# A two-layer adaLN kernel on one core: the hand-over from attention to the experts, and the normalisation in front of it

## The chip, the cores and the metric

The kernel runs on one core of one Trainium2 chip. The metric is the time of one execution in microseconds on the device; less is better. All data are float32, apart from small float16 tables of zeros, ones and counts that the routing uses. The engines named below are PE (TensorE, matrix products), DVE (VectorE), ACT (ScalarE), POOL (GpSimd) and SP (SyncE, which here only issues DMAs). PE needs two records in the trace for one float32 product, so the counts of float32 products in the profile are twice those in the code.

## The reference, cut to what matters

`x` has 4 batches of 1024 tokens of 256 features. Every layer has an attention part and a feed-forward part, each behind a layer norm that is modulated by rows computed from a condition `c`:

```python
mod = (silu(c) @ wmod).reshape(4, 6, 1, 256)   # shift, scale, gate, for both parts
h = layernorm(x) * (1 + ca) + sa
x = x + ga * L0_attn(h, queries, combiners)     # linear attention, 4 heads of 64
h = layernorm(x) * (1 + cb) + sb
x = x + gb * L0_ffn(h, W1, b1, W2, b2, Wr, br)  # 8 experts, the best 2 of each token
mod = (silu(c1) @ wmod1).reshape(4, 6, 1, 256)  # "layer 1's modulation rows"
x = x + ga1 * L1_attn(...)                      # a gated MLP over chunks of 128 tokens, in sequence
x = x + gb1 * L1_ffn(...)                       # 8 single matrices, the best 2 of each token
```

The attention has no softmax, so for each batch it comes down to a Gram matrix of `h` per head, a product with the combiners and one with the queries, and then one 128x128 product per 128 tokens. In `L0_ffn` an expert is a 256x1024 matrix with a ReLU and a 1024x256 matrix. Which two experts a token gets depends on the data.

## The kernel before, in words

**Tiles.** The 4096 tokens are 32 tiles of 128: 8 chunks `c` for each of 4 batches `b`, in the order `c * 4 + b`. Chunks 0 to 3 (`g = 0`, "half 0") are tiles 0 to 15, chunks 4 to 7 (`g = 1`, "half 1") are tiles 16 to 31.

**The prologue.** It ends at about 104 us. It is a list of pieces, each with an engine, an estimated duration, what it comes after, the buffer slots that it holds, and a rank. The class `Plan` simulates the engines with these estimates, always taking the ready piece of lowest rank, and writes the pieces out in the order in which the simulation began them; the engines then run exactly that order (`manual_schedule`). `FIRSTS[b]` and `SECONDS[b]` are the ranks of a batch's two halves of work:

- `first_half(b)`: `normalised` (below), `to_features` (transposes on PE, shift and scale on ACT), `to_tokens` (transposed back), the Gram matrix, `head_t1` (two products of a 128x128 block-diagonal matrix `gd` with the combiners, line 1289) and `head_m`.
- `second_half(b)`: the products with `md`, the sums into `x_sb` (DVE), `normalised` again, `to_features`, the router's product (line 194, in four column tiles of 32), and `route` on DVE, which picks two experts per token. Batch 3 (`SPLIT`) routes its two halves apart, four tiles each; the others route eight tiles at once. The tokens are stored to `h_rows` in DRAM, one DMA for each `g` of a batch, and `mark` stores their routing data.

`normalised` does for each group of four tiles: `bn_stats` and `bn_aggr` for each tile (lines 1097 and 1098, DVE), then the variance plus epsilon into `ln_v` (line 1101, DVE), the square root (line 1105, ACT), a reciprocal and one Newton step (lines 1109 to 1116, DVE), and last the scaling of the tiles, two on POOL (line 1126) and two on ACT (line 1128). There are 16 such groups: four batches, two halves of chunks, two norms.

**The hand-over.** Each half's routing table is turned round by `turn` (PE), copied by `turned` (ACT, `pairs`) and `counted` (DVE, `more`). When both are there, `bases` (PE) and `begin` (ACT) give blocks 0 and 1 their limits; both belong to expert 7. `sought(j)` finds the 128 tokens of block `j`: `reach` (DVE, line 817, one instruction for each half), `look` (PE, line 847), `find` (DVE, lines 860 and 869). `first_block` then fetches the rows of block 0 with an indirect DMA on POOL, which waits for `find` and for all entries of the list `stores`, turns them (PE, line 1562), copies them (ACT, line 1674), and starts the products `hidden` (line 1610) and `values` (line 1634). Meanwhile DVE works out which expert each later block has: `whole_blocks`, `with_halves`, `close_staged`, then `across` on PE (line 749), `limits`, and `sought(2)`. Two kinds of PE work fill holes: 12 pieces of one product and 12 of two products of a tile of ones at low rank (`kept_busy`, line 1033), some of them with an earliest planned time (`at`), and layer 1's modulation rows (`modulation_rows`, line 1523): 12 products, each 4 rows wide, of 256 columns.

**The experts of layer 0.** A program-order loop runs blocks 0 to `turning - 1`, with `turning = J - LATE`, and a second plan those up to `passed = J - SPARE`. A block is 16 products for `hidden` and 8 for `values`. The weights come by indirect DMA on POOL (line 353) into two buffers each for W1 and W2; both pairs are filled with expert 7's before the loop. In the loop, POOL issues the rows of block 2 first and then block 2's W1. `once(j)` does single things at given blocks; at block 5 it stores the modulation rows to DRAM.

Layer 1 follows from about 590 us, from a plan of its own.

## Time and profile before

| what | value |
|---|---|
| median of 8 runs | 1077.8 us (1075.57 to 1080.38) |
| the profiled execution | 1075.64 us, its span 1073.9 us |
| PE busy over the span | 1038.1 us (97%) |
| DVE, ACT, POOL busy over the span | 602.0, 396.8, 426.7 us |
| granted TensorE clock | 0.995 of full speed |
| the chain that ended last | 33% of the span on PE, 8% on DVE |
| 1408 records of `p_h` (line 1610) and 1008 of `p_y` (line 1634) | 275 and 382 ns each |

Busy times are unions of intervals. The ends of matmuls are modelled, so a full PE column means that PE was not left waiting, not that the array worked at its peak. Idle time before an instruction is shown in square brackets with what ended it. Times within the span count from its start.

### The profile page before, as it was taken

To read this page: it belongs to the slowest core of one execution; us is meant where nothing else is said; L and a number is where in the kernel's file an instruction comes from. 1 tells how busy PE (TensorE), PEld (TensorE's weight loads), DVE (VectorE), ACT (ScalarE), POOL (GpSimd) and SP (SyncE) were. 2 spreads that over 40 slices of the span, in tenths; PEclk is the share of its full clock that TensorE was granted. 3 is DMA by queue.
4 is the path that set the end of the run, shared out by engine and by line. 5 is a ranking of instruction groups with operands and counts; after the bars stand their busy time and mean duration, and the time that the engine had idled before them with its cause. 6 is when DMAs were issued, how large, how long until landed. Compare 5 with 4: busy or idle time off the path is not lost. (4 is left out here: it accounts for less than half of the span.)

```text
span 1073.9 us, 18875 instructions
## 1 busy us (share of the span) xinstructions
PE 1038.1 (97%) x6193; PEld 802.0 (75%) x6193; DVE 602.0 (56%) x2323; ACT 396.8 (37%) x1077; POOL 426.7 (40%) x509
## 2 busy tenths in 40 slices
PE   8999999999999999999999999999999999998993
PEld 5885899989989989989999465564656566646751
DVE  7997343232222222221165588878778726698767
ACT  5766332323332332322253433432224325342521
POOL 3211466546555555544453010110106321574644
PEclk9999999999999999999999999999999999999998
DMA  8604626576543726464171222221014322352534
GB/s 284 239 21 110 216 67 212 203 275 198 178 160 119 237 66 201 120 215 153 31 260 40 72 60 64 62 81 48 18 34 140 111 66 77 106 169 76 161 111 147
DMA packets 94255, 139.81 MB, mean 130 GB/s; under 512 B 31009, under 2 KB 69933, under 8 KB 89542
## 3 DMA queue, kind: packets, MB, share of 16 engines
q0 software_dynamic: 30080, 68.89, 20.3%
q1 hardware_dynamic: 62966, 68.04, 19.9%
q10 hardware_dynamic: 1104, 1.58, 0.4%
q8 instruction: 53, 0.87, 0.3%
q14 instruction: 52, 0.43, 0.1%
HBM read 202.22 MB, written 29.17 MB: 215 GB/s over the span
## 5 line engine op out<-in xcount | busy, mean ns | idle before, releaser
L1622 ACT ACTIVATE hid<-p_h,w 128x128 f32<-128x128 f32 x504 | 144.0, 369 | 300.7 <-issue 194.5
L1634 PE MATMUL p_y<-w,hid 128*128 128x256 f32 x1008 | 230.5, 382 | 0.7 <-DMA w<-in_W,g_wrow 0.7
L2430 PE MATMUL p_u<-hT,a 128*128 128x512 f32 x512 | 229.3, 595 | 0.9 <-ACTq L2395 0.9
L1634 PEld LDWEIGHTS p_y<-w,hid 128*128 128x128 f32 x1008 | 186.9, 190 | 24.6 <-issue 1.0
L2430 PEld LDWEIGHTS p_u<-hT,a 128*128 128x128 f32 x512 | 94.9, 190 | 102.6 <-issue 92.8
L1610 PEld LDWEIGHTS p_h<-xTq,w 128*128 128x128 f32 x1408 | 163.3, 192 | 1.7
L1610 PE MATMUL p_h<-xTq,w 128*128 128x128 f32 x1408 | 164.5, 275 | 0.0
L353 POOL DMA_INDIRECT w<-in_W,g_wrow x124 | 125.7, 1013 | 68.6 <-ACT hid L1622 43.8
L1645 DVE TENSOR_TENSOR y<-p_y,w 128x256 f32<-128x256 f32 x64 | 27.2, 424 | 193.3 <-PE p_y L1634 193.2
L914 POOL DMA_INDIRECT y<-y,g_dest x64 | 66.3, 1036 | 131.4 <-DVE y L1645 72.4
L2478 PE MATMUL p_f<-a,hf 128*128 128x256 f32 x512 | 116.9, 380 | 0.0
L2478 PEld LDWEIGHTS p_f<-a,hf 128*128 128x128 f32 x512 | 95.9, 190 | 18.7 <-issue 6.4
L2526 POOL TENSOR_TENSOR x_sb<-x_sb,step 128x256 f32<-128x256 f32 x32 | 24.8, 775 | 207.4 <-DVE step L2519 164.5
L860 DVE TENSOR_SCALAR_CACHE_REDUCE g_hits<-pm_counts,g_nth 128x128 f16<-128x128 f32 x68 | 23.6, 347 | 89.5 <-PE pm_counts L847 86.3
L1610 PE MATMUL p_h<-xT,w 128*128 128x128 f32 x608 | 71.3, 276 | 0.4 <-DVE xT L1567 0.4
L1610 PEld LDWEIGHTS p_h<-xT,w 128*128 128x128 f32 x608 | 70.3, 192 | 1.2 <-DVE xT L1567 0.6
L2442 ACT ACTIVATE hf<-p_u,decay 128x512 f32<-128x512 f32 x56 | 38.3, 685 | 76.9 <-PE p_u L2430 73.4
L2738 PE MATMUL p_e<-ew,xT 128*128 x256 | 65.0, 385 | 0.3 <-ACT y L2748 0.3
L2446 DVE SCALAR_TENSOR_TENSOR hf<-p_u,decay,hf 128x512 f32<-128x512 f32 x56 | 41.8, 746 | 21.6 <-PE p_u L2430 8.3
L2089 DVE TENSOR_TENSOR h<-h,mod 128x256 f32<-128x256 f32 x128 | 51.4, 423 | 4.1 <-ACT h L2079 2.1
L353 POOL DMA_INDIRECT xg<-ga_rows,ga_row x36 | 34.3, 952 | 45.9 <-DVE ga_row L869 16.4
L2738 PEld LDWEIGHTS p_e<-ew,xT 128*128 128x128 f32 x256 | 44.8, 190 | 8.7 <-issue 2.9
(420 smaller groups left out, 1340.3 us busy)
## 6 DMA issues: line engine op xcount, KB each, us to landing
yg<-y SPq DMA_DIRECT2D x32, 256.0 KB
xTq<-square SPq DMA_DIRECT2D x176, 32.0 KB
ew<-in_W SPq DMA_DIRECT2D x16, 288.0 KB
ga_y<-y SPq DMA_DIRECT2D x36, 128.0 KB
half<-in_W SPq DMA_DIRECT2D x16, 257.0 KB
x_sb<-in_x SPq DMA_DIRECT2D x8, 512.0 KB
h_rows<-xn SPq DMA_DIRECT2D x8, 512.0 KB
hT<-square SPq DMA_DIRECT2D x128, 32.0 KB
```

Of the source, the lines that this page charges most:

```text
L353: return nc.gpsimd.indirect_dma_start(out=dst, out_offset=None, in_=table, in_offset=bass.IndirectOffsetOnAxis(ap=index, axis=0), bounds_c ...
L914: nc.gpsimd.indirect_dma_start(out=table if parts == 1 else table.rearrange("r (i d) -> (r i) d", i=parts), out_offset=bass.IndirectOffset ...
L1610: nc.tensor.matmul(p1[:, i, :], lhsT=w1[:, k * H + m * P : k * H + (m + 1) * P], rhs=xT[k], start=(k == 0), stop=(k == KD - 1),)
L1622: nc.scalar.activation(hid[:, m, :], p1[:, i, :], AF.Relu, bias=w1buf[j % 2][:, KD * H + m : KD * H + m + 1],)
L1634: nc.tensor.matmul(p2, lhsT=hid[:, m, :], rhs=w2[:, m * D : (m + 1) * D], start=(m == 0), stop=(m == KH - 1),)
L1645: nc.vector.tensor_tensor(y, p2, w2buf[j % 2][:, KH * D :], ALU.add)
L2089: nc.vector.tensor_tensor(h, h, mods1[(sc, sh)[i]][:, b, :], (ALU.mult, ALU.add)[i])
L2430: nc.tensor.matmul(pu, lhsT=a[:, k, m * P : (m + 1) * P], rhs=made["n1", c, "hT"][:, k, :, :], start=(k == 0), stop=(k == KD - 1),)
L2442: nc.scalar.activation(made[key, m], made[key, m, 0], AF.Silu, scale=decays[c])
L2446: nc.vector.scalar_tensor_tensor(h, made[key, m, 1], decays[c], h, ALU.mult, ALU.mult)
L2478: nc.tensor.matmul(made[key, "p2", b], lhsT=made[key, m][:, b * P : (b + 1) * P], rhs=a1[:, m, :], start=(m == 0), stop=(m == KH - 1),)
L2738: nc.tensor.matmul(made[key, "p2"], lhsT=made[key, "xT"][:, k, :], rhs=ew_flat[:, bass.ds(made[key, "at"] + k * D, D)], start=(k == 0), st ...
```

## The change

In `normalised`, epsilon is added by the square root itself (as its bias) and inside the Newton step, so the separate `ln_v` instruction is gone, and POOL scales three of the four tiles of each group. The ranks `FIRSTS` and `SECONDS` and several estimated durations are new, so the whole order of the prologue is worked out anew. `head_t1` multiplies only the two diagonal 64x64 quadrants. Blocks 0 and 1 are sought among half 0's pairs alone: `first_bases` and `begin` follow half 0's `turn`, a table `absent` stands in for half 1 in `look`, and the first two fetches wait for half 0's stores only. As expert 7 may have fewer than 256 pairs in half 0, `short` corrects the later blocks for it, and `J` grows by one, as do `LATE` and `SPARE`. The six modulation rows are computed in three column tiles at partitions 0, 32 and 64, in four rounds of three products, and stored by six DMAs.

```diff
-LATE = 16
-SPARE = 8
+LATE = 17
+SPARE = 9
...
-    rows1 = half1[:B, : 6 * D].rearrange("p (i d) -> p i d", d=D)
+    rows1 = {}
+    for i, (t, q) in {2: (0, 0), 0: (1, 0), 1: (2, 0), 5: (0, 1), 3: (1, 1), 4: (2, 1)}.items():
+        rows1[i] = (32 * t, q, half1[32 * t : 32 * t + B, q * D : (q + 1) * D])
...
-            self.n, self.J, self.name = n, blocks_of(n) + (name == "g0"), name
+            self.n, self.J, self.name = n, blocks_of(n) + 2 * (name == "g0"), name
...
+        def first_bases(self, pool):
+
+            K = self.K
+            pt = psum(pool, [K, self.halves], "pm_bases")
+            for h, of in enumerate((below16, same16)):
+                nc.tensor.matmul(
+                    pt[:, h : h + 1],
+                    lhsT=of[:K, :K],
+                    rhs=self.pairs[:K, 0, :1],
+                    start=True,
+                    stop=True,
+                )
+            return pt
...
+            nc.vector.tensor_scalar(
+                self.short,
+                self.pt[:, 2, E - 1 :],
+                float(2 * P),
+                float(2 * P),
+                ALU.min,
+                ALU.subtract,
+            )
+            nc.vector.tensor_tensor(
+                whole[:, :, E - 1 :],
+                whole[:, :, E - 1 :],
+                self.short.unsqueeze(1).to_broadcast([P, 3, 1]),
+                ALU.subtract,
             )
...
+            nc.vector.tensor_scalar(
+                origin[:, 0:1], self.short, -1.0 / P, None, ALU.mult
+            )
+            own7 = origin[:, 2 * E - 1 :: E]
+            nc.vector.tensor_scalar(own7, own7, origin[:, 0:1], None, ALU.add)
...
-        def look(self, pool, reached):
+        def look(self, pool, reached, first=False):
...
-                    rhs=self.more[: self.K, h, :],
+                    rhs=(self.absent if first and h else self.more[:, h, :])[: self.K],
...
     def by_gpsimd(k, b, g, i):
-        return i < 2
+        return i < 3
...
-            if c == cs[-1]:
-                v = tiles["v", key] = pa.tile([P, n], F32, tag="ln_v", name="ln_v", bufs=6)
-                nc.vector.tensor_scalar(v, tiles["mv", key][:, :, 1], EPS, None, ALU.add)
...
-            nc.scalar.activation(y, tiles["v", key], AF.Sqrt)
+            nc.scalar.activation(y, tiles["mv", key][:, :, 1], AF.Sqrt, bias=eps)
...
-            nc.vector.tensor_tensor(t, t, v, ALU.mult)
+            nc.vector.scalar_tensor_tensor(t, mv[:, :, 1], EPS, t, ALU.add, ALU.mult)
...
-    FIRSTS, SECONDS, SPLIT = [0, 1.3, 2.42, 2.65], [1.28, 4.7, 2.66, 4.55], 3
+    FIRSTS, SECONDS, SPLIT = [0, 1.48, 1.79, 1.8], [1.64, 5.29, 3.2, 4.59], 3
...
-                nc.tensor.matmul(
-                    p1[:, j, :],
-                    lhsT=gd[:, j, :],
-                    rhs=comb[:, j, :, :].rearrange("p a g -> p (a g)"),
+                for r in (slice(0, 64), slice(64, P)):
+                    nc.tensor.matmul(
+                        p1[r, j, :],
+                        lhsT=gd[r, j, r],
+                        rhs=comb[r, j, :, :].rearrange("p a g -> p (a g)"),
...
+        if half == 0:
+            ps2 = plan.slot("p1")
...
+            m2 = plan(PE, 0.15, first_bases, after=[of_batch["turned"]], holds=[ps2], rank=-1.6)
+            begun = plan(
+                ACT,
+                0.35,
+                lambda: g0.begin(tiles["first bases"]),
+                after=[m2],
...
+        for col in range(2):
+            for k in range(KD):
+                def mm(col=col, k=k):
+                    for i, (at, q, _) in rows1.items():
+                        if q == col:
+                            nc.tensor.matmul(
+                                tiles["rows1"][at : at + B, q * D : (q + 1) * D],
+                                lhsT=sT1[:, k, :B],
+                                rhs=tiles["wm1"][:, k, i * D : (i + 1) * D],
...
-            POOL, 1.0, lambda: g0.fetch(xgbuf[0], h_rows, 0), after=[found, *stores], rank=-1.6, lag=2.9
+            POOL, 1.0, lambda: g0.fetch(xgbuf[0], h_rows, 0), after=[found, *stores[0]], rank=-1.6, lag=2.9
...
-    d = plan(DVE, 1.6, lambda: g0.limits(pa), after=[m, bs], holds=[ps], rank=-1.0)
+    d = plan(DVE, 1.6, lambda: g0.limits(pa), after=[m, bs, found[0], found[1]], holds=[ps], rank=-1.0)
...
-            nc.sync.dma_start(mod_rows1, rows1)
+            for i in range(6):
+                nc.sync.dma_start(mod_rows1[:, i, :], rows1[i][2])
```

## The prediction

> **What bounds the kernel now.** I read the page first. PE has work almost throughout:
>
> ```profile
> PE 1038.1 (97%) x6193; PEld 802.0 (75%) x6193; DVE 602.0 (56%) x2323; ACT 396.8 (37%) x1077; POOL 426.7 (40%) x509
> ```
>
> PE's idle gaps, added up from its timeline, come to under 3 us between 104 and 594 us. So the experts of layer 0 start when the prologue lets them, and run at PE's pace: whatever moves their start moves the end by as much. The change is all ahead of that start (after it stand six small stores for one). What matters is what bounds the prologue. The busy time by stretches says:
>
> ```profile
> 8.00:20.00 12.00, 10.73 (x75) 7.79 (x74) 10.90 (x51) 6.56 (x12) 4.73 (x41) 1.00 1.09 360
> 20.00:40.00 20.00, 18.76 (x247) 15.83 (x245) 18.36 (x75) 14.03 (x29) 4.39 (x8) 1.00 0.88 331
> 40.00:60.00 20.00, 18.86 (x232) 16.05 (x233) 18.15 (x79) 16.41 (x35) 5.62 (x10) 1.00 0.20 58
> 60.00:80.00 20.00, 19.77 (x250) 17.62 (x247) 17.88 (x67) 14.05 (x29) 3.29 (x6) 1.00 0.08 28
> 80.00:95.00 15.00, 13.45 (x140) 8.79 (x139) 12.75 (x61) 12.39 (x26) 2.20 (x4) 1.00 0.66 156
> ```
>
> The third pair is DVE: 90% in each stretch. The rest is not waiting: in its timeline from 8.0 to 94.9 us all gaps over 0.1 us add up to 0.8 us, and the others are the 0.03 to 0.04 us between dependent instructions. PE looks as full, but 16.8 us of it before 110 us are products of ones (line 1033) and its ends are modelled. DVE bounds the prologue. Its relevant groups between 8 and 95 us:
>
> ```profile
> L1097 DVE BATCH_NORM_STATS2 ln_st<-x_sb 128x6 f32<-128x256 f32 x60 | 24.6, 410 | 0.7 <-DMA x_sb<-in_x 0.4
> ...
> L1113 DVE TENSOR_TENSOR ln_t<-ln_t,ln_v 128x4 f32<-128x4 f32 x16 | 2.8, 173 | 0.5
> ...
> L1101 DVE TENSOR_SCALAR ln_v<-ln_mv 128x4 f32<-128x4 f32 x15 | 2.5, 170 | 0.5
> ```
>
> Then the hand-over, from the timelines of DVE, PE and POOL:
>
> ```profile
> 86.62 0.46 DVE L426 TENSOR_TENSOR r_hit<-r_hit,rank 128x64 f32<-128x64 f32 x1
> ...
> 88.43 0.23 DVE L426 TENSOR_TENSOR r_hit<-r_hit,rank 128x64 f32<-128x64 f32 x1
> ...
> 94.54 0.17 DVE L446 TENSOR_TENSOR g_both<-g_one 128x32 f16<-128x32 f16 x1
> ...
> 96.17 0.74 DVE L817 TENSOR_SCALAR g_reached<-count,g_limit 128x128 f16<-128x128 f16 x4 [0.43 <-ACT g_limit L603]
> ...
> 102.85 0.32 DVE L700 TENSOR_TENSOR g_diagonal<-ident,g_of_p 128x152 f32<-128x152 f32 x1
> ```
>
> ```profile
> 97.46 4.91 PE L1523 MATMUL pm_mod<-wmod,sT 128*4 128x256 f32 x22
> 102.30 0.51 PE L1562 MATMUL pm_x<-ident,xg 128*128 128x128 f32 x2
> ...
> 103.71 1.05 PE L1610 MATMUL p_h<-xg,w 128*128 128x128 f32 x8
> 104.60 0.42 PE L749 MATMUL pm_blocks<-g_diagonal,ones 128*128 128x152 f32 x2
> ...
> 116.90 3.84 PE L1610 MATMUL p_h<-xT,w 128*128 128x128 f32 x32 [0.40 <-DVE xT L1567]
> ```
>
> ```profile
> 98.80 1.15 POOL L353 DMA_INDIRECT xg<-h_rows,g_row  x1 [11.25 <-DVE g_blocks_i L625]
> ...
> 109.54 0.95 POOL L353 DMA_INDIRECT xg<-h_rows,g_row  x1 [8.34 <-DVE g_row L869]
> 110.80 1.03 POOL L353 DMA_INDIRECT w<-in_W,g_wrow  x1 [0.30 <-issue]
> ```
>
> The last route ends at 94.71 us, blocks are sought from 96.17, block 0's rows are asked for at 98.80 and land at 101.8 (DMA completions), PE turns them at 102.30, right behind the modulation rows, and block 0 starts at 103.71. Block 2 (116.90) is the first with new weights: asked for at 110.80, landed at 116.6.
>
> **The prologue, by parts.** *Line 1101 goes.* Where it stands, the next independent DVE instruction starts 295 ns after `bn_aggr`; elsewhere 99 ns after. So it takes 196 ns, 16 times: **-3.1 us**, in an engine that does not wait. The Newton step swaps a TENSOR_TENSOR (173 ns) for the form of its neighbours (163 to 176 ns): 0. The memset of epsilon falls into DVE's idle 3.25 us at 2 us: 0.
>
> *POOL scales 16 more tiles.* They take 563 ns each on POOL, idle for 65 of these 87 us, and leave ACT, where they take 598. Price on DVE: a two-input instruction that meets a scaling lasts longer (the 0.46 above against 0.23; in Newton steps 0.26 to 0.35 against 0.16). I add up some 1.2 us over today's 32 tiles, so 16 more cost **+0.6 us** (0 if they meet none, 1.2 if twice as often). `bn_stats`, the largest row, takes 409 ns under a scaling and 409 without. The Trainium skill (SBUF — State Buffer, "Who interferes with whom") speaks against the move more strongly: of a two-input DVE instruction and a GpSimd one that reads SBUF, the second fully blocks. Taken as a stop of half a scaling, 0.28 us, for each of the 16, that would be 4.5 us, an estimate; the trace shows far less, as most of DVE's time has one SBUF input. A group's scaling now ends after three POOL tiles (1.8 us). In the last group it ended 2.2 us after Newton, as ACT had other work (POOL 86.46 to 87.56, ACT until 88.37): -0.4 to +0.6, I take 0, hidden by routes that DVE does meanwhile; uncovered it would be 0.6.
>
> *`head_t1`.* Four records of 216 ns a batch become eight. No row shows quadrants that also split the rows; with column tiles the Gram products (line 1256) start in pairs 7 ns apart. Paired, it is 0.9 us as now; serial, 0.9 more per batch on PE, covered by PE's filling and not by DVE's work. I take 0, between -0.4 (the planner's estimates) and +0.9, as only the one before batch 0's products could reach the path. The Trainium skill (TensorEngine Tiling (Array Packing), "Gotcha 1: PSUM Pressure") says that different row tiles cannot use one PSUM bank at the same time, and both quadrants here write one; that would be the serial case, four times 0.9 us on PE.
>
> *The new order.* The trace cannot show it. DVE has only 0.8 us of gaps to win; it can lose what a wrong order opens. I take 0 here, and treat the loss as rivals. Prologue: -3.1 + 0.6 = **-2.5 us** (-3.9 to +1.5).
>
> **The hand-over.** *Search.* Half 0's last route ends at 91.95. From there, `turn` (to 92.64), ACT's copy (93.32), two products and ACT's `begin` (0.42) are done by about 94.2, while DVE does the last route until 94.71. So `reach` can follow at 94.75 instead of 96.17: -1.4. `find`, fetch (98.80 becomes 97.4; found and stores set it) and landing (100.4) move with it. The last store of half 1 landed at 97.8, so waiting for all would have stopped the fetch there; those of half 0 had landed by 96.5.
>
> *Modulation rows.* 24 records of 216 ns, 5.2 us. Line 194 shows column tiles: four records 7 ns apart, then 113. Eight rounds of three are about 1.9 us, and fit between `look` and the landing. So PE no longer stands behind them: turned at 100.4 rather than 102.30, block 0 at about 101.35 instead of 103.71, **-2.4 us**. Serial, they would still end at about 101 and take 0.5 of it back. The two late fillings with fixed planned times (98.9 and 99.4 us, four products of 0.216) can now fall behind block 0's start: 0 to 0.9 us, I take **+0.2**.
>
> *Block 2's weights.* They have 0.3 us of slack, so the gain only lasts if they come earlier too. POOL asks for them behind block 2's rows, which wait for `find` of block 2 (ended 109.27). On that path DVE gets four more small instructions (0.8 us at the 0.2 us spacing of `close_staged`), against the 1.4 gained: the diagonal is ready at 102.5, not 103.17. `across` follows at a gap between PE's pieces of 0.9 us, `limits` and `reach` take 2.0 (105.06 to 106.99), so about 105.5; `look` stands behind 4.7 us of block 0's products (103.71 to 108.40), thus at 106.05. Both agree on `find` some 2.3 us earlier. If `across` meets its gaps badly, 0.3 to 1 us is left. I take **-2.2** for the search with all behind it (-2.4 to -0.3).
>
> *The rest.* `J - LATE` stays 56 and `J - SPARE` 64, so the same blocks run. SP issues five more DMAs at block 5, 0.36 us each; behind them the next are those of block 8, over 15 us on: 0, and at most 1.8 if uncovered.
>
> Sum: -2.5 - 2.2 + 0.2 = **-4.5 us** against the profiled 1075.64, which is 2.2 under the median of 1077.8: 1071.1 there, **1073.3** as a median.
>
> **The rivals.**
> - *Weights hold block 2* (0.12). `find` of block 2 stays late as DVE's closing work, not the search, sets it. For it: 0.3 us of slack. Against: 1.4 gained before 0.8 added. -2.5 - 0.3 + 0.2: 1075.2.
> - *Prologue no shorter* (0.15). The freed DVE time turns into gaps, as PE or ACT feeds it too late: ACT was busy all of 80 to 90 us. Against: it loses 9 us of work. -2.2 + 0.2: 1075.8.
> - *Both* (0.07): the change then does not do what it says, and -0.1 remains: 1077.7.
> - *Slower: batch 1 comes last* (0.11). Its second half now ranks 0.70 behind batch 3's, before 0.15. A last group needs 5.9 us from Newton (86.19) to its route (92.07); DVE covered that with two routes. If batch 3's are done by then, DVE stands idle for up to 5.9 us, and one route of eight tiles closes both halves, so that the early search finds nothing to overlap. -2.5 + 5.9 + 0.4 (longer route) + 0.8 (added DVE work) - 0.5 (modulation rows): +4.1, 1081.9. It decides from 1.8 us of idle time on; beyond 0.2% from 4.0.
>
> **How the numbers follow.** The forecast has 0.55, its own range 1071.3 to 1075.2. 0.2% (2.2 us) is about what a measurement of this kernel can tell from no change. Faster: 0.53 of the forecast, two thirds of the weights case and 0.06 of the third: 0.67. Slower: the last rival, 0.11. Same: the rest. The low end adds the best ends (-3.1 - 2.4, and ACT's relief): 1070.5. The high end, 1078.0, leaves out the slower rival and a few hundredths on each side.
>
> **What would show it.** No `ln_v` row; DVE gaps up to the last route still under 1.5 us; that route ending near 92.2; `reach` within 0.1 us of it; modulation records in threes; block 0's first `p_h` near 98.8 and block 2's near 112.1. Wrong if DVE shows gaps of microseconds before the last route, if that one has eight tiles, if block 2's W1 lands after its `xT` by over 1 us, or if products of ones stand behind block 0's start.

## The result and the profile after

The changed kernel takes 1081.56 us in the median (1079.06 to 1083.73, 13 runs), the kernel before, on the same chip, 1077.55: the ratio is **1.0036, 95% interval 1.0026 to 1.0047**. It is slower by about 4 us, where 4.5 us less were forecast. The profiled execution took 1079.26 us, its span is 1077.5 us, 3.6 us more than before. Beside the later experiments the same kernel was measured on another chip, with the same ratio.

The page's line on the engines shows that PE still has work almost throughout:

```profile
PE 1039.5 (96%) x6212; PEld 802.5 (74%) x6212; DVE 599.7 (56%) x2312; ACT 389.7 (36%) x1061; POOL 435.0 (40%) x526
```

The shift is there before the experts of layer 0 get under way: the first `y` stands at 122.44 us, 5.1 later than before, and from there to 356 us every block is 5.1 to 5.2 later. (Later parts give 1.5 us of it back; I did not trace where.) The busy time by stretches, with PE, PEld, DVE, ACT, POOL, then the granted clock, the DMA share and GB/s:

```profile
8.00:20.00 12.00, 10.15 (x58) 6.68 (x57) 9.71 (x44) 3.92 (x7) 5.95 (x44) 0.86 1.09 352
20.00:40.00 20.00, 20.00 (x264) 16.42 (x263) 17.86 (x73) 12.98 (x26) 6.53 (x12) 1.00 0.88 328
40.00:60.00 20.00, 19.73 (x241) 16.65 (x239) 17.61 (x71) 16.09 (x32) 6.53 (x12) 1.00 0.23 70
60.00:80.00 20.00, 19.57 (x246) 16.89 (x246) 17.03 (x61) 10.80 (x22) 6.53 (x12) 1.00 0.01 2
...
104.00:110.00 6.00, 4.46 (x20) 4.08 (x21) 0.00 (x0) 0.37 (x1) 0.42 (x1) 0.50 0.13 39
```

DVE, the third pair, is busy for less of these first four stretches than before, and the last route yet ends no earlier: what `ln_v` freed has become waiting. The clock is at half speed in the last row, and already 0.86 in the first. DVE's groups between 8 and 95 us, and its longer waits in the timeline (in brackets, with what ended them):

```profile
L1145 DVE BATCH_NORM_STATS2 ln_st<-x_sb 128x6 f32<-128x256 f32 x60 | 24.2, 404 | 0.9 <-DMA x_sb<-in_x 0.7
...
L1371 DVE TENSOR_TENSOR md<-pm_m,ga 64x128 f32<-64x128 f32 x8 | 2.3, 289 | 3.1 <-PE pm_m L1358 3.0
```

```profile
16.22 0.17 DVE L1111 COPY modT<-pm_modT 128x8 f32<-128x8 f32 x1 [0.59 <-PE pm_modT L1098]
18.02 0.41 DVE L340 TENSOR_SCALAR g_sign<-pm_mod 4x256 f32<-4x256 f32 x1 [0.69 <-PE pm_mod L327]
...
60.73 0.59 DVE L1371 TENSOR_TENSOR md<-pm_m,ga 64x128 f32<-64x128 f32 x2 [1.37 <-PE pm_m L1358]
```

The waits over 0.15 us between 7 and 95 us add up to 5.0 us: 0.72 for the first loads, 1.28 for PE at 16 and 17 us, when its clock was low, and 3.0 for `pm_m` ahead of `md`, where the new order asks for a product that PE has not done yet. The hand-over, from the timelines of DVE, PE and POOL:

```profile
95.18 0.17 DVE L449 TENSOR_TENSOR g_both<-g_one 128x32 f16<-128x32 f16 x1
95.27 0.73 DVE L863 TENSOR_SCALAR g_reached<-count,g_limit 128x128 f16<-128x128 f16 x4
...
97.69 0.16 DVE L915 SCALAR_TENSOR_TENSOR g_row<-pm_counts,g_count 128x1 int32<-128x1 f32 x1
```

```profile
97.27 1.47 PE L1590 MATMUL pm_mod<-wmod,sT 128*4 128x256 f32 x18
99.21 0.61 PE L1590 MATMUL pm_mod<-wmod,sT 128*4 128x256 f32 x6 [0.47 <-ACT half L353]
...
104.99 0.70 PE L1631 MATMUL pm_x<-ident,xg 128*128 128x128 f32 x2 [3.55 <-DMA xg<-h_rows,g_row]
...
106.73 3.62 PE L1679 MATMUL p_h<-xg,w 128*128 128x128 f32 x16
110.15 0.62 PE L795 MATMUL pm_blocks<-g_diagonal,ones 128*128 128x154 f32 x2
110.61 1.95 PE L1679 MATMUL p_h<-xg,w 128*128 128x128 f32 x16
```

```profile
102.02 1.15 POOL L356 DMA_INDIRECT xg<-h_rows,g_row  x1 [15.78 <-DVE g_origin L735]
...
114.64 0.94 POOL L356 DMA_INDIRECT xg<-h_rows,g_row  x1 [10.22 <-DVE g_row L915]
```

`reach` starts right behind the last route, as forecast, and both row lists are there at 97.85. But POOL fetches at 102.02. The bracket blames a DVE instruction of that moment, which is not what the fetch needs; the instruction's own semaphores are those of the `h_rows` DMAs, all of them, half 1's too, and the last lands at 101.0 (DMA completions), at which POOL's wait ends. In every profile in which stores hold the fetch it leaves 1.0 to 1.1 us behind that landing; in that of before it did, too (97.8 and 98.80). So PE waits 3.55 us with nothing left to do, and then runs block 0's first 16 records of `p_h` (8 products) in 3.62 us; the next 16, a moment later, take 1.95. SP's timeline shows where the stores went, first after, then before:

```profile
85.47 1.62 SPq L1498 DMA_DIRECT2D h_rows<-xn  x2
88.25 0.36 SPq L1483 DMA_DIRECT2D h_rows<-g_meta  x1
90.04 0.36 SPq L1498 DMA_DIRECT2D h_rows<-xn  x1
91.05 0.36 SPq L1483 DMA_DIRECT2D h_rows<-g_meta  x1
91.68 1.82 SPq L1498 DMA_DIRECT2D h_rows<-xn  x2
93.60 0.69 SPq L1483 DMA_DIRECT2D h_rows<-g_meta  x1
```

```profile
84.45 0.36 SPq L1449 DMA_DIRECT2D h_rows<-xn  x1
87.37 0.36 SPq L1436 DMA_DIRECT2D h_rows<-g_meta  x1
87.82 1.93 SPq L1449 DMA_DIRECT2D h_rows<-xn  x2
90.20 3.13 SPq L1436 DMA_DIRECT2D h_rows<-g_meta  x2
93.43 0.45 SPq L1449 DMA_DIRECT2D h_rows<-xn  x1
```

After has five 512 KB stores from 85.47 to 93.14 us, before four from 84.45 to 93.43. Issue of the last to its landing took 7.4 us after (93.61 to 101.0) and 4.4 before (93.43 to 97.8).

### The profile page after: what moved, and what is told of

It is laid out like the page before. It is cut to its first block, busy times and chain, and to the rows that moved or that the text cites. A ratio compares the mean times of both kernels' runs of the same rounds, so it can differ in the third digit from the quotient of the medians.

```text
span 1077.5 us, 18918 instructions
## 1 busy us (share of the span) xinstructions
PE 1039.5 (96%) x6212; PEld 802.5 (74%) x6212; DVE 599.7 (56%) x2312; ACT 389.7 (36%) x1061; POOL 435.0 (40%) x526
## 3 DMA queue, kind: packets, MB, share of 16 engines
q0 software_dynamic: 30080, 68.89, 20.1%
## 5 line engine op out<-in xcount | busy, mean ns | idle before, releaser
L2500 PEld LDWEIGHTS p_u<-hT,a 128*128 128x128 f32 x512 | 94.9, 190 | 102.6 <-issue 92.8
L2548 PEld LDWEIGHTS p_f<-a,hf 128*128 128x128 f32 x512 | 95.8, 190 | 19.4 <-issue 6.4
```

Of the source, the lines that this page charges most:

```text
L2500: nc.tensor.matmul(pu, lhsT=a[:, k, m * P : (m + 1) * P], rhs=made["n1", c, "hT"][:, k, :, :], start=(k == 0), stop=(k == KD - 1),)
L2548: nc.tensor.matmul(made[key, "p2", b], lhsT=made[key, m][:, b * P : (b + 1) * P], rhs=a1[:, m, :], start=(m == 0), stop=(m == KH - 1),)
```

## The experiments

The theory that I set out with had three links: (i) block 0's fetch waits for every store of `h_rows` ahead of it in the program, and the new order lets them land late; (ii) PE, with the modulation rows shortened, then has nothing to do, its clock halves, and block 0 pays; (iii) in the new order, and with POOL's third tile, DVE's waits eat what `ln_v` saved. Rivals: the third tile on POOL, the early drop of the clock, the search itself. Each ratio below is to runs of the kernel before on the same chip.

One table carries the readings of all profiles: when the last `h_rows` DMA that the fetch waits for was issued and landed, when the fetch left, how long PE waited right ahead of block 0's transposes, how long block 0's first 16 records of `p_h` took, and the time from the fetch to the first `y`.

| run | issued | landed | fetch | PE waits | 16 records | fetch to `y` | ratio (95%) |
|---|---|---|---|---|---|---|---|
| before | 93.43 | 97.8 | 98.80 | 0 | 2.2 | 18.6 | 1 |
| after | 93.61 | 101.0 | 102.02 | 3.55 | 3.6 | 20.4 | 1.0036 (1.0026-1.0047) |
| after_again | 94.01 | 103.3 | 104.30 | 5.46 | 2.9 | 19.6 | 1.0035 (1.0018-1.0052) |
| b_lnv | 92.41 | 98.4 | 99.42 | 1.03 | 2.2 | 18.0 | 0.9990 (0.9978-1.0002) |
| a_old_prologue | 96.88 | 102.6 | 103.68 | 1.91 | 3.6 | 20.9 | 1.0020 (1.0010-1.0031) |
| a_warm | 94.33 | 103.5 | 104.58 | 1.92 | 3.6 | 20.9 | 1.0062 (1.0039-1.0085) |
| a_two_same | 97.91 | 107.7 | 108.73 | 6.24 | 3.6 | 20.6 | 1.0058 (1.0039-1.0077) |
| a_late | 90.74 | 95.1 | 96.70 | 0 | 2.05 | 18.7 | 0.9980 (0.9967-0.9992) |
| a_warm0 | 92.49 | 100.2 | 101.22 | 3.88 | 3.6 | 20.8 | 1.0047 (1.0034-1.0060) |
| b_warm0 | 94.43 | 98.5 | 99.55 | 0 | 2.2 | 18.8 | 0.9987 (0.9973-1.0000) |
| c_late_warm0 | 89.35 | 93.4 | 96.17 | 0 | 2.05 | 18.9 | 0.9958 (0.9945-0.9971) |
| a_oldrows | 96.13 | 104.5 | 105.55 | 4.06 | 3.9 | 22.3 | 1.0056 (1.0038-1.0075) |
| a_late_warm0 | 91.57 | 95.8 | 97.58 | 0 | 2.05 | 18.7 | 0.9975 (0.9961-0.9989) |
| c_late_v | 91.61 | 95.2 | 98.43 | 0 | 2.05 | 18.9 | 0.9964 (0.9951-0.9977) |
| c_nolate | 92.38 | 96.6 | 97.67 | 0.46 | 1.95 | 18.5 | 0.9958 (0.9944-0.9973) |
| a_warm0_oldrows | 93.14 | 102.1 | 103.09 | 4.43 | 3.4 | 21.1 | 1.0047 (1.0031-1.0063) |
| c_late_three | 89.60 | 93.1 | 96.24 | 0 | 2.05 | 18.7 | 0.9944 (0.9922-0.9966) |
| c_late_cold | 90.43 | 94.7 | 97.26 | 0 | 2.05 | 18.6 | 0.9958 (0.9941-0.9975) |
| d_order | 93.01 | 99.0 | 100.09 | 2.22 | 3.4 | 20.1 | 1.0012 (0.9985-1.0040) |
| d_order_warm0 | 93.73 | 99.5 | 100.59 | 2.05 | 1.95 | 18.5 | 1.0006 (0.9985-1.0027) |

### `b_lnv`: the additions of epsilon gone, nothing else

```diff
-                nc.vector.tensor_scalar(v, tiles["mv", key][:, :, 1], EPS, None, ALU.add)
-            nc.scalar.activation(y, tiles["v", key], AF.Sqrt)
+            nc.scalar.activation(y, tiles["mv", key][:, :, 1], AF.Sqrt, bias=eps)
-            nc.vector.tensor_tensor(t, t, v, ALU.mult)
+            nc.vector.scalar_tensor_tensor(t, mv[:, :, 1], EPS, t, ALU.add, ALU.mult)
```

> The kernel before with one edit: the 16 additions of epsilon (`ln_v`, 196 ns each on DVE) are folded into the square root's bias and into the next DVE step, in the order of before. If DVE bounds the prologue as I said (under 1 us of gaps between 8 and 94.9), the last route ends 2.5 to 3.1 us earlier, near 91.9, and the time falls by 2 to 3.1 us, to 0.997 to 0.998 of before. Rival, by which the saving of 3.1 us is not to be had at all since DVE then waits for ACT's square roots or PE's rows: the last route ends after 94, gaps of 2 us and more stand on DVE, and the time is within 0.1% of before.

Measured: 1078.19 against 1079.55 us, 0.9990, between the two forecasts and not told apart from no change. In its profile the first loads came 1.19 us later than in that of before (DVE waits 1.59 and 0.40 us for `x_sb` near 7.5), and yet the last route ends 1.0 us earlier: 2.2 of the 3.1 us arrived, most of the rest went into two waits for `ln_y` (0.58 and 0.70 us, before 0.29 and 0.27). The row list is there 1.0 us earlier too (96.88 against 97.90). But POOL's fetch comes later than before:

```profile
99.42 1.15 POOL L353 DMA_INDIRECT xg<-h_rows,g_row  x1 [12.86 <-DVE g_up L662]
```

The last store was issued 1.0 us earlier than before and landed 0.6 later, at 98.4. So already before the change DVE and the stores ended together (97.9 and 97.8); freeing DVE alone leaves the stores as the bound.

### `a_old_prologue`: only the search and the short rows

```diff
-        return i < 3
+        return i < 2
+                nc.vector.tensor_scalar(v, tiles["mv", key][:, :, 1], EPS, None, ALU.add)
...
-    FIRSTS, SECONDS, SPLIT = [0, 1.48, 1.79, 1.8], [1.64, 5.29, 3.2, 4.59], 3
+    FIRSTS, SECONDS, SPLIT = [0, 1.3, 2.42, 2.65], [1.28, 4.7, 2.66, 4.55], 3
```

> The kernel after with the normalisation, the combiner's products, their order and their split between ACT and POOL put back as they were before: what is left of the change is the search of blocks 0 and 1 from half 0 and the modulation rows in column tiles. Theory (the new order of the prologue, with its late and bunched stores and DVE gaps, makes the loss): the last route ends at 94.7 as before, block 0's rows are found near 97.1 in place of 97.9, the fetch still waits for the last store of both halves (landed 97.8 before) and leaves at 98.0 to 98.8, so 0 to 1 us is won at block 0, and the time is 0.5 to 2 us under before and 5 to 6 us under after. Rival (the wait is for half 0's stores only, as I had predicted): the fetch leaves at 97.2 and block 0 starts 1.5 to 2.4 us earlier than before. Second rival (the search or the rows in column tiles make the loss): the time is 2 to 4 us above before, as that of after is.

Measured 1.0020: a miss for all three, closest to the second rival. The profile tells how: the clock was low from 15 to 21 us, the whole prologue came 3.2 to 3.5 us later, the last store landed at 102.6, and PE, without the long rows, had 1.9 us with nothing to do; block 0 ran at half speed. With the stores this late, the early search has nothing to win, and the long rows that had filled PE's wait are gone. How much of the loss is due to that and how much to the late prologue, this run does not tell.

### `a_warm` and `a_oldrows`: something for PE to do ahead of block 0

```diff
         def turn():
+            busy(3.6)
             kept0["pt"] = turn_rows(0)
```

> The kernel after with 16 products of ones issued on PE right ahead of block 0's turn, in the time in which PE waits for block 0's rows; their result is used by nothing. Theory (PE's 3.55 us of waiting drops its clock to 0.50, and block 0's 16 products take 0.215 us each in place of 0.11): the clock stays at or near 1.00 from 104 to 110, block 0's first layer takes 1.8 us and not 3.6, and the time falls by 1.5 to 2.2 us against after. Rival (the lower clock is of no account since W1 or block 2's rows end last behind it): block 0 is shorter by the same amount, but block 2 starts no earlier, and the time is within 0.05% of after.

`a_oldrows` has `modulation_rows`, `rows1` and `modulation1` of the kernel before:

```diff
-    modulation_rows(m0)
+    modulation_rows(m0, (0, 1, 2))
```

> The kernel after, in its order, with layer 1's modulation rows computed as before (24 products on 4 partitions one after another, some 3.4 us longer on PE). Theory (the shorter rows leave PE without work for 3.55 us ahead of block 0, which halves its clock; before, the rows filled that time): the fetch leaves at 102 as in after, PE waits under 1 us ahead of block 0's turn, its clock stays near 1.00 from 104 to 110, block 0's 16 products take 1.8 to 2.2 us in place of 3.6, and the time falls by 1 to 2 us, to 1.002 to 1.0027 of before. Rival (the clock at block 0 is of no account, or the longer rows delay block 0 by as much): 1.0033 to 1.005 of before.

Both missed: 1.0062 and 1.0056, if anything slower than after. In both the fetch itself left later (104.58 and 105.55 in place of 102.02), so that PE ran out of work again, for 1.92 and 4.06 us, and block 0 was at half speed as before. They show nothing about a kept clock.

### `a_two_same`: the new order with two tiles on POOL

```diff
-            if by_gpsimd(*key, i):
+            if i < 2:
```

> The kernel after, in the same order, with the third tile of each group normalised on ACT as before, not on POOL. If POOL's third tile is what holds the new prologue up (DVE slowed by POOL's scalings beside it, PE waiting for xn), the last route ends 1 to 2.5 us earlier than 95.35, and the time falls by 1 to 2.5 us against after. If it is the new order itself (the `md` pieces waiting for `pm_m`, the stores in one bunch), the route ends within 0.5 us of 95.35, later rather than earlier where ACT is now the longer, and the time is within 0.7 us of after.

Measured 1.0058, no better than after: the third tile on POOL is not what holds the new prologue up. The last route ends at 99.45, 4.1 us later than in after and outside both forecasts: the first loads came 1.2 us later, the early clock stayed low for twice as long, and with two tiles on POOL, in an order that was made for three, DVE waits 1.9 us more for `ln_y`. Its stretch from 95 to 100 us is the plainest view of bunched stores, transfers busy throughout (1.24) at 122 GB/s:

```profile
95.00:100.00 5.00, 4.89 (x44) 2.71 (x44) 4.35 (x25) 3.07 (x9) 0.00 (x0) 1.00 1.24 122
```

### `a_late`: the fetch freed from the last stores

```diff
+                if (b, g) in ((1, 1), (3, 1)):
+                    postponed.append((store, back, [slot], 3.2))
...
+    plan("SP", 0.4, early0, rank=-3.0, at=57.0)
...
+    for do, when, holds, lag in postponed:
+        plan("SP", 0.4, do, after=[*when, fetched], holds=holds, rank=5.0, lag=lag)
```

The last mark is postponed alike. `early0` and its like store raw `x` to the same rows beforehand; no block reads these before the real ones are there.

> The kernel after, in its order, with the two last stores of half 1's rows and the last mark issued behind the fetches of blocks 0 and 1 (512 KB stores of raw x into the same rows go ahead, at a time when the transfers are few). Theory (block 0's fetch waits for every store of `h_rows` that stands ahead of it in the program, half 1's too, and the bunched stores land last, at 101.0, against 97.4 for the search): the fetch leaves at 98.0 to 98.8 in place of 102.0, PE no longer waits 3.55 us, its clock stays at 1.00, block 0 begins near 103 and loses no 1.8 us, and the time falls by 4 to 5.5 us, to 0.9985 to 0.9998 of before. Rival (the loss is in the order of the prologue and in the early clock, whatever the fetch waits for): the route ends at 95.3 as in after, and the time is within 1 us of after (1.003 of before). Second rival (the time was only moved: block 2's rows now wait for the late stores): block 0 is earlier, block 2 is not, and 1 to 2 us are won.

Measured 0.9980, 6 us under after: the theory's number and a little more. Its POOL and PE, in their timelines:

```profile
96.70 1.15 POOL L356 DMA_INDIRECT xg<-h_rows,g_row  x1 [11.45 <-DVE g_hits L906]
...
108.12 0.94 POOL L356 DMA_INDIRECT xg<-h_rows,g_row  x1 [9.02 <-DMA h_rows<-xn]
```

```profile
100.29 0.39 PE L1663 MATMUL pm_x<-ident,xg 128*128 128x128 f32 x2
...
101.42 2.05 PE L1711 MATMUL p_h<-xg,w 128*128 128x128 f32 x16
```

The fetch follows the row list (96.42) and not the stores; PE has no wait ahead of the rows; block 0 starts 5.3 us earlier than after and runs at full speed. DVE's waits for `md` are as in after (3.2 against 3.0 us), but in this profile the early clock did not fall, and the last route ends 1.0 us earlier (94.37). So 1.0 of the 5.3 us is not the fetch's; `a_late_warm0` against `a_warm0` (below), with the early clock kept in both, shows the same step, 0.9975 against 1.0047. The second rival is seen, but small: block 2's fetch now waits for a late store, by its bracket, and still leaves 6.5 us before that of after.

### `a_warm0`, `b_warm0`, `c_late_cold`: the early clock

```diff
                 pt = tiles["pt", key, k] = psum(ps_m, [P, 4, P], "pm_t")
+                if "warmed" not in tiles:
+                    tiles["warmed"] = True
+                    for _ in range(6):
+                        nc.tensor.matmul(pt.rearrange("p a b -> p (a b)"), lhsT=busy16[:, :P], rhs=busy16, start=True, stop=True)
```

> The kernel after with 6 products of ones (1.3 us of PE) right ahead of the first group's transposes, where PE waits for POOL's and ACT's first `xn`; they go into the tile that the transposes overwrite. Theory (PE's 1.9 us of idle time between 8 and 14 us is what drops its clock to 0.50 from 15 to 19; at 1.0 us, as in before, and at 1.66, as in the kernel with `ln_v` alone gone, it stayed at 1.00): the clock stays at 1.00, DVE's waits of 0.59 and 0.69 us for `pm_modT` and `pm_mod` go, every store and the last route are 1.3 to 2 us earlier, and the time falls by 1 to 2 us, to about 1.002 of before. Rival (the clock falls for another reason): it is at 0.50 again between 14 and 20, and the time is that of after, 1.0036 of before, or 0.3 us above.

> The kernel before with the same 6 products at the same place. Theory (the runs of before differ by whether the first loads come late enough to drop the clock; those with a mean clock of 0.989 to 0.991 are 2 to 3 us longer than those with 0.995): the slower runs go, and the median falls by 0.5 to 1.5 us, 0.9985 to 0.9995 of before. Rival (the spread comes from elsewhere): the ratio is 1.000 and the spread of the runs stays 4 us.

> The fastest so far without the 6 products of ones: what the early clock is worth where nothing behind it makes the loss larger. Theory: in runs in which the first loads come late the clock falls to 0.50 near 15 and the stores and the route come 2 to 3 us later, in the others nothing changes: the median is 0.5 to 2 us above the fastest, 0.9963 to 0.9977, and the runs spread by 4 us in place of 2. Rival (in before's order PE idles too little for that): 0.9953 to 0.996.

The clock did stay at 1.00, and the waits for `pm_modT` and `pm_mod` went. But after gained nothing by it: 1.0047, as the last store still landed at 100.2 and PE waited 3.88 us:

```profile
104.20 0.70 PE L1641 MATMUL pm_x<-ident,xg 128*128 128x128 f32 x2 [3.88 <-DMA xg<-h_rows,g_row]
```

The kernel before gained 1.4 us, if anything (the interval reaches 1.0000). The fast version of the next section (`c_late_warm0`) without these products, `c_late_cold`, has the same 0.9958 as with them. That is its rival's number, but not for the rival's reason, as in its profile the clock did fall to 0.50, from 15.7 to 19.1 us. So the early clock is not the cause; that theory of mine fell.

### `c_late_warm0`, `a_late_warm0`, `c_nolate`: before's order with the rest

`c_late_warm0` is the kernel after with the split of the normalisation, the ranks and the combiner's products of before, `ln_v` still gone, the late stores and the six products. `a_late_warm0` has the new prologue instead. `c_nolate` is `c_late_warm0` with all stores in their place. Against `a_late`, `c_late_warm0` is, beside the six products and the planner's estimated durations:

```diff
-        return i < 3
+        return i < 2
...
-    FIRSTS, SECONDS, SPLIT = [0, 1.48, 1.79, 1.8], [1.64, 5.29, 3.2, 4.59], 3
+    FIRSTS, SECONDS, SPLIT = [0, 1.3, 2.42, 2.65], [1.28, 4.7, 2.66, 4.55], 3
...
-                for r in (slice(0, 64), slice(64, P)):
+                nc.tensor.matmul(
+                    p1[:, j, :],
```

> Before's order and split of the normalisation, with `ln_v` gone, the search of blocks 0 and 1 from half 0, the modulation rows in column tiles, the late stores of half 1 as in the run that only postpones them, and the 6 products of ones ahead of the first transposes. Theory (a fetch that waits for half 0's stores alone gets what I had predicted for it): last route near 92.5 to 93.5, block 0's rows found near 95.5, the fetch at 96 to 97 in place of 98.8, block 0 begins 2 to 2.7 us earlier than before, and the time is 2 to 3.5 us under before (0.9968 to 0.998). Rival (the weights or the rows of block 2 hold what is won, as in the first rival of the prediction): block 0 earlier by the same, block 2 not, and the time within 1 us of before.

> The kernel after with the late stores of half 1 and the 6 products of ones ahead of the first transposes: against the fastest so far (0.9958 of before) it differs only in the order, the split and the combiner's quadrants of the new prologue. If the new order is worth nothing by itself, as I had taken it, the ratio is 0.9955 to 0.9965. If its gaps on DVE (0.5, 0.2, 1.4 and 0.95 us for `md`, and POOL's third tile beside DVE) are its price, the route ends 0.5 to 1 us later than in the fastest and the ratio is 0.9967 to 0.998.

> The fastest so far with all stores in their place again, ahead of the fetches. Theory (the wait for every store is what holds the fetch, in before's order too): the search is done near 96, but the last store lands between 97 and 98.5, the fetch leaves at 98 to 99.5, PE waits for it 1.5 us or more with the short modulation rows and its clock falls in block 0, and the time is 0.9985 to 1.0015 of before. Rival (the stores are of no account, the search and `ln_v` made the gain): 0.9955 to 0.997.

Measured 0.9958, 0.9975 and 0.9958. The first gained a little more than the theory said, the second came as it said: the forecast's gain is there once the fetch is free, and the new prologue (order, split and quadrants together) costs some 2 us, by intervals that overlap. The third was a miss that taught more. In before's order the fetch waits for every store, too, and that costs almost nothing:

```profile
97.66 1.15 POOL L356 DMA_INDIRECT xg<-h_rows,g_row  x1 [11.14 <-DVE g_odd L679]
```

```profile
100.64 0.50 PE L1639 MATMUL pm_x<-ident,xg 128*128 128x128 f32 x2 [0.46 <-DMA xg<-h_rows,g_row]
...
102.29 1.95 PE L1687 MATMUL p_h<-xg,w 128*128 128x128 f32 x16
```

Its last store was issued at 92.38, as late as that of `a_warm0` (92.49), but landed 4.2 us later and not 7.7: at 96.6, 1 us behind the row list. `a_warm0` and `c_nolate` have the same wait, the same search, the same short rows and the same early clock, and stand at 1.0047 and 0.9958, with intervals far apart. What differs is the prologue's order, POOL's third tile and the quadrants.

### `c_late_v` and `c_late_three`: single terms where nothing else holds the fetch

`c_late_v` puts the 16 additions back into `c_late_warm0`, by the edit of `b_lnv` undone; `c_late_three` gives the third tile to POOL in the same order:

```diff
-            if by_gpsimd(*key, i):
+            if i < 3:
```

> The fastest so far with the 16 `ln_v` additions on DVE put back, in the same order. Theory (where no store holds the fetch, DVE sets the time of the search, and 16 x 196 ns show): the route ends 2.2 to 3.1 us later, the fetch leaves at 98.4 to 99.2 in place of 96.2, and the time rises by 2 to 3 us, to 0.9975 to 0.9985 of before. Rival (DVE's waits for ACT's square roots and for PE give it all back): the rise is under 1 us, 0.996 to 0.9966.

> The fastest so far (0.9958) with the third tile of each group normalised on POOL and not on ACT, in the same order. I had priced that at +0.6 us (16 tiles, DVE slowed by POOL beside it). If that holds, the route ends 0.4 to 1 us later, and the ratio is 0.9960 to 0.9968. Rival (three scalings of 0.55 us one behind the other on POOL make `xn` late, and the transposes, `md` and DVE wait for it): the route ends 2 us or more later, with DVE gaps for `pm_m`, 0.9975 or more. Other rival (ACT was what DVE waited for, in two waits of 0.58 us for `ln_y`): these go, and the ratio is under 0.9956.

`c_late_v`: 0.9964 against 0.9958, nearer to the rival; the intervals allow up to 3 us. In the profiles the fetch leaves 2.3 us later, of which 0.8 are later first loads. `c_late_three`: 0.9944 (0.9922 to 0.9966), the lowest of all, and the last route ends where it did without the third tile (93.91 and 93.84). The last rival's number came, though only 0.2 us of the two waits for `ln_y` went. No cost of that tile is seen in this order; the intervals leave room for some 1.5 us.

### `after_again` and `a_warm0_oldrows`

The first is the changed kernel, unedited; the second joins the edits of `a_warm0` and `a_oldrows`:

```diff
+                    for _ in range(6):
...
-    modulation_rows(m0)
+    modulation_rows(m0, (0, 1, 2))
```

> The changed kernel once more, beside the runs below, since chips differ in how late the first loads come (DVE waits 0.4 to 1.9 us for `x_sb` near 7.5). Theory: where that wait is 1.2 us or more, PE's idle time between 8 and 14 grows past 1.8 us, the clock stays at 0.50 longer than in the first profile, the stores are issued 1 to 3 us later, and the ratio is 1.004 to 1.006; where it is 0.7, 1.003 to 1.005. In both, the last store lands 8 to 10 us after its issue, the fetch leaves 1.0 us behind it, PE idles over 3 us and block 0 runs at half clock. Rival (the first profile was a chance, and the loss has no one place): the fetch leaves under 100 or block 0 runs at full clock, with the same ratio.

> The kernel after with the 6 products of ones ahead of the first transposes and with the modulation rows computed as before, 3.4 us longer on PE: the early clock is taken out of the question, which was what spoiled the run with the old rows alone. Theory (PE's idle time ahead of block 0 drops the clock, and the shorter rows made that time): early clock 1.00; last store lands at 100 to 101, fetch at 101 to 102; PE works until 103.5, waits 1 to 1.5 us, and its clock stays at 1.00 through block 0; fetch to first `y` takes 18.0 to 18.9 us in place of 20.4 to 20.9; the time is 1.8 to 2.2 us under that with the products of ones alone (1.0047), so 1.0025 to 1.003 of before. Rival (not the idle time but the stores or the gather slow PE there): half speed again from 104 to 110, 1.0045 or more.

The changed kernel had 1.0035 on another chip, with every link in its profile again: last mark issued at 94.01, landed at 103.3, PE waiting 5.46 us. The long rows with the early clock kept had 1.0047, like `a_warm0` without them, where 1.0025 to 1.003 was forecast. PE ran out of work at 101.6 (the last two row products, four records, stood behind the transposes), the last store landed at 102.1, 1.9 us later than in `a_warm0`, and PE waited 4.43 us all the same. What the half clock costs by itself could not be had by filling PE's time.

### `d_order` and `d_order_warm0`: every edit, before's order

```diff
-        return i < 3
+        return i < 2
...
-            if by_gpsimd(*key, i):
+            if i < 3:
...
-    FIRSTS, SECONDS, SPLIT = [0, 1.48, 1.79, 1.8], [1.64, 5.29, 3.2, 4.59], 3
+    FIRSTS, SECONDS, SPLIT = [0, 1.3, 2.42, 2.65], [1.28, 4.7, 2.66, 4.55], 3
...
-        t = plan(PE, 0.5, head_t1, after=[d], holds=[ps, t1s], rank=rank - 0.3)
+        t = plan(PE, 0.9, head_t1, after=[d], holds=[ps, t1s], rank=rank - 0.3)
```

The estimated durations of the statistics and the scaling are put back as well, and with `by_gpsimd` they only serve the planner; nothing that the engines execute differs from the kernel after but the order (and, in the second, the six products).

> The whole change but for its order: every edit of the kernel after is there (`ln_v` gone, three tiles on POOL, the combiner's quadrants, the search from half 0, the rows in column tiles), and only the planner's ranks, costs and the number of tiles that it assumes on POOL are as before, so that the prologue runs in before's order. Theory (the loss is the new order's, through its bunched stores): the last store lands 4 to 6 us after its issue and not 8 to 10, the fetch leaves at 97.5 to 100, block 0 runs at full clock in most runs, and the ratio is 0.996 to 0.9995 of before, 4 us and more under after (1.0035). Rival (the edits themselves, the third tile on POOL or the quadrants, make the loss, or the early clock does): 1.002 or more.

> The same with the 6 products of ones ahead of the first transposes, to be set beside after with them (1.0047) and beside the run without the third tile and the quadrants (0.9958). Theory: the fetch leaves at 97.5 to 98.5, PE waits under 2 us for block 0's rows and keeps its clock, 0.994 to 0.9965. Rival: 0.999 or more, if the third tile or the quadrants cost anything where the order does not hide it.

Measured 1.0012 and 1.0006, neither told apart from before, nor, by their intervals, `d_order` from after. The first lies between its two forecasts, the second in its rival's range: taken as they stand, they show no gain. The chip that these two fell on takes 1109.5 us for the kernel before, 30 more than the others, and PE idles more on it all through (7.3 us in `d_order` from 125 to 600 us, 1.4 in `c_nolate`; 42.7 and 23.9 behind that), so I set these ratios beside the rest only with reserve. The profiles still say something: the last store landed 6.0 and 5.8 us after its issue, not 7.4 to 9.8 as in every kernel with the new order and all stores in their place. But that was late enough (99.0 and 99.5, with block 0's row list at 96.4 and 97.1) for PE to wait 2.2 and 2.05 us, and in the first block 0 ran at half speed.

## Why the prediction was wrong

**The step that failed** is the sentence "those of half 0 had landed by 96.5", with the one on the new order, "I take 0 here". I took the landing times of the stores as fixed and the fetch as waiting for half 0's alone. Neither held. `after=stores[0]` only orders the plan; in the profile after, the fetch waits for every write to the tensor `h_rows` that stands ahead of it in the program. And the landing depends on how the order spaces the stores: in the profile after, half 0's own last store landed at 99.3, so that waiting for half 0's alone would still have held the fetch until 100.3. `a_late` does both at once, it takes half 1's last stores out of the wait and out of the bunch, and that is worth 6 us. I had the rule at hand, "waiting for all would have stopped the fetch there", and used it as an assurance and not as a rival.

**The sum, step by step**, in the profile after:

- *Prologue, -2.5 forecast:* the last route ends at 95.35, not 92.2; +0.6 against before. `ln_v` is gone, but new waits of DVE took its place. My sign for that, gaps of microseconds, came true; the rival "prologue no shorter" held in substance, as a term and not as the whole. `c_late_v` puts what the additions are worth at 0.6 us, at most 3.
- *POOL's third tile, +0.6:* about right as DVE's time (see below), and not seen in the kernel's: with the third tile the ratio was 0.9944, without it 0.9958 (`c_late_three`, `c_late_warm0`).
- *`head_t1`, 0:* right. 32 records of quadrants take 4.6 us of PE in the prologue, 16 full ones took 4.4, and in three of the four batches the second quadrant of a pair starts 6 or 7 ns behind the first, so the two do run beside each other. That speaks against the serial reading of the Trainium skill (TensorEngine Tiling (Array Packing), "Gotcha 1: PSUM Pressure").
- *Search, -2.4:* the mechanism was right. `reach` follows the last route within 0.1 us, and block 0's rows are found 2.1 us behind that. Where the fetch was free, it left at once.
- *Modulation rows:* right in length, 2.1 us. What I missed is what they had hidden: before, 4.9 us of them filled PE's wait for the rows, and its clock stayed at 1.00.
- *Block 0:* forecast near 98.8, came at 106.73. Of the 7.9 us, 2.8 are the later prologue (a free fetch would have left at 97.7, by the 2.4 us from `reach` to fetch in `a_late`, and not at 94.9), 4.3 the fetch's wait for stores (97.7 to 102.0), 0.8 the gather and the slower transposes (4.7 us from the fetch to block 0, forecast 3.9). From there to the first `y` it takes 2.1 us more than before, 1.4 in the first 16 records and 0.7 behind them, so that +3.0 at block 0's start becomes +5.1. At full clock the same code takes 13.9 us (`a_late`), here 15.7: 1.8 of the 2.1 us go with the half clock.
- *Slower rival, 1081.9:* the number was close and the mechanism was not this one. The last route still has four tiles (128x32), and no DVE wait of 1.8 us stands ahead of it.
- *The range:* its low end of 1070.5 is not reached by its own best terms, -3.9 and -2.4, which give 1071.5. That had no part in the miss.

**POOL beside DVE.** In the profile after, a Newton step on DVE with two inputs in SBUF that begins beside a scaling ends within 10 ns of the scaling's end. Undisturbed it takes 0.16 us; here:

```profile
45.44 0.56 POOL L1171 TENSOR_SCALAR xn<-x_sb,ln_y,ln_m 128x256 f32<-128x256 f32 x1 [3.36 <-DVE ln_y L1154]
45.66 0.34 DVE L1158 SCALAR_TENSOR_TENSOR ln_t<-ln_mv,ln_t 128x4 f32<-128x4 f32 x1
```

What the two-input instructions lose in this way adds up to 1.7 us after and 1.0 before, close to the 0.6 forecast. That agrees with the rule of the Trainium skill (SBUF — State Buffer, "Who interferes with whom"), by which the two shut each other out. The estimate of 4.5 us that I drew from it was wrong in taking every one of the 16 scalings to stop DVE; most meet no such instruction.

**The clock.** The runs sort themselves by PE's wait ahead of block 0: up to 1.0 us, full speed in all; from 3.55 us on, half speed in all, at least at first; at 1.9 to 2.2 us, half in three and full in one. The time from the fetch to the first `y` is 18.0 to 18.9 us in the one group and 19.6 to 22.3 in the other. It is a sorting and one kind of intervention: taking the wait away (`a_late`) took the half speed away, but also the late rows. The Trainium skill (TensorE: Matmul & The Clock Gate, "Part 1: The HAM clock gate (the "warmup" mystery)") tells of an activity window of some 3.4 us that runs free of the kernel, and of half speed after an idle one. The traces agree with the window: in each of the 20, all changes of the granted clock are whole multiples of 3.41 us apart, at a place that differs from run to run. They do not agree that the window must be idle throughout. What sorts the runs is PE's idle time within one such stretch: behind 20 us, every stretch at full clock with more than 1.9 us of it is followed by half clock, and none with less is (1.83 us was kept ahead of block 0 in `a_warm0_oldrows`, 1.91 was not in `a_old_prologue`). That settles the cases near 2 us. In `d_order` 1.5 of the 2.22 us of waiting and all of a later wait of 0.80 fall into one stretch, with PE busy for 1.10 of 3.42 us; in `d_order_warm0` the end of a stretch cuts the wait of 2.05 us in two:

```profile
101.52:104.94 3.42, 1.10 (x7) 0.91 (x8) 0.68 (x4) 0.37 (x1) 0.94 (x1) 1.00 0.29 77
104.94:108.35 3.41, 3.41 (x18) 3.41 (x17) 0.00 (x0) 0.25 (x1) 0.00 (x0) 0.50 0.00 0
```

```profile
99.43:102.85 3.42, 2.12 (x12) 0.80 (x9) 3.02 (x20) 2.02 (x5) 1.96 (x2) 1.00 0.11 23
102.85:106.26 3.41, 1.91 (x14) 1.72 (x15) 0.28 (x2) 0.37 (x1) 0.14 (x1) 1.00 0.18 55
106.26:109.67 3.41, 3.41 (x29) 3.35 (x29) 2.00 (x11) 1.58 (x6) 0.00 (x0) 1.00 0.00 0
```

This is a sorting too, and no run tried it. Ahead of 20 us it does not hold: the clock fell there after stretches with 1.3 us idle (after).

**What stays open.** That the order makes the stores land late is what the profiles show: the last store lands 4.1 to 6.0 us after its issue in all seven with before's order and all stores in their place, 7.4 to 9.8 in all seven with the new order, and `d_order` differs from after in nothing else. That the order alone makes the time is not shown: the two runs that undid it alone had no gain, on a chip of its own. A cost of the quadrants that the order does not hide stays possible, as only kernels without them came to 0.9958 or less. Why a landing takes 7 to 10 us was not tried either.

## What to carry to other kernels

Here a transfer's wait was set by the tensor, and not by the rows that the code means: before counting on an earlier fetch, list the semaphores that it waits for, and when each writer lands. Landing times belong to the order of the work: the last store took 4 to 6 us to land in one order and 7 to 10 in the other, so no fixed lag prices it. And an edit that shortens work which only filled a wait can cost time, since it leaves the wait bare and PE's clock with it. Much of the change was sound: `ln_v` gone, the third tile, the early search and the short rows, in before's order, with the last stores of the other half behind the fetch and the six products of ones, give 0.9944 of the kernel before (0.9922 to 0.9966). The new order and the quadrants are not in that.

## What the runs showed that I had not expected

- Bunched stores can move less in all than one alone. A 1 KB packet of a row store took 47 ns on average when a store ran alone (80 to 82 us in the profile after, 246 GB/s), 120 ns at 92 to 94, and 150 to 160 in `a_two_same` at 96 to 100; from 95 to 100 the transfers there moved 122 GB/s while busy all the time. Loads had moved 328 GB/s from 20 to 40 us in the profile after. Each batch's marks, 8-byte pieces in the same rows of 1032 bytes, fall in between; whether they are the reason was not tried.
- The same kernel's first loads come 0.4 to 1.9 us late by run and chip (DVE's wait near 7.5), which alone moves every time of the prologue in a single profile. The landing delay (issue to landing) and the fetch-to-`y` time do not contain it, and so told more than absolute times.
- PE lost its clock near 15 us after idling 1.85 us between 8 and 14 (after), and kept it after 1.87 (`b_lnv`). There the idle sum alone does not decide.
